# Layer 3's attention with smaller projection pieces, one a step, and router logits on VectorE

## The chip, the core and the metric

The kernel runs on one core of a Trainium2 chip, in one launch. The metric is the device time in microseconds. A core has five engines with queues of their own: PE (TensorE, matrix products into PSUM), DVE (VectorE, elementwise work and copies out of PSUM), ACT (ScalarE, activation functions), POOL (GpSimd) and SP, which here issues DMAs. PSUM has eight banks; one holds 128 x 512 numbers of 32 bits. All data are float32.

## The reference

Four layers in a row work on 8 samples of 256 channels by 1024 positions: two of convolutions, one of attention with a sparse feed-forward part, and layer 3, which the change concerns. A sample of layer 3 is 1024 tokens of 256 channels:

```python
t = t + _L3_attn_ref(_ln_t(t), qkv_w, qkv_b, proj_w, proj_b)
t = t + _L3_ffn_ref(_ln_t(t), router_w, w1, b1, w2, b2)
# attention: 8 heads of 32 channels, no softmax
scores = jnp.einsum('bnhd,bmhd->bhnm', q, k) * scale
s = jnp.square(scores + 5.0)
attn = s / jnp.sum(s, axis=-1, keepdims=True)
out = jnp.einsum('bhnm,bmhd->bnhd', attn, v).reshape(B, N, D) @ proj_w.T + proj_b
# feed-forward: 8 experts, two for each token
probs = jax.nn.softmax(tokens @ router_w.T, axis=-1)
rw, re = jax.lax.top_k(probs, 2)
# out = tokens + sum over the chosen experts of weight * (gelu(tokens @ w1 + b1) @ w2 + b2)
```

## The kernel before

Each layer is a Python generator; a layer's head (its loads, and what needs no space of the layer before) is issued beside the end of the layer before it. A list scheduler then orders the instructions of each engine: program order is its priority, an instruction can move ahead when it is ready earlier, and `pinned` ties one behind what was issued before it on its engine. Waits on tiles, and on space that another tile had, are set by the framework. Engines work their own queues in order.

**Attention of layer 3** is `fast3`. A sample has 32 steps: 2 halves of the queries (`hh`, 512 tokens each), 2 groups of four heads (`c`), 8 blocks of 128 keys (`kt`). In a step, four score matmuls (L2686), one for each head and each in 32 rows of the array, fill two pairs of PSUM banks, (s); ACT squares each pair (L2692) into `e`; one step later, four value matmuls (L2670), each in 32 columns of the array, add into the bank `A`. After eight steps `A` is multiplied by the inverse sums `r` into `o` (L2675), and after sixteen, the output projection (a whole pair, L78 and L2681) is added to the sample in `x`. PSUM holds three pairs with the tag S and two banks for A; every other user of PSUM in this stage takes a pair of S as well, through `pair` or `bank`.

Beside the steps of sample b, `between(b)` issues in this order: the routing of sample b - 1 (`Routes.route`: a norm, a transpose of the normed sample on PE (L2398), logits on PE (L78, mo_l), softmax, the two best experts by comparisons, and places by a running count with two small matmuls (mo_n)); the norm of sample b + 1 (`norm`: load, statistics on DVE, Ln and Exp on ACT, scaling, transposes into `xn`); and its projections (`projections`: q, k and v, then the denominators. Since no softmax is used, a row's sum follows from the Gram matrix of the keys, G, from the product of it with q, and from a sum over a head's channels, D.) `spread` deals them out evenly over 33 steps; a piece of projections takes a whole pair, and up to 16 matmul instructions. After sample 0's projections `routes.fill` presets the 19 MB lists that tokens are later sorted into. Sorting of a group of samples (`sort`) runs beside the samples 4 and 7.

Ahead of the first step come sample 0's transposes and projections. In the space that `own["k1"]` gets, and that the last layer's tiles leave, lies `kt`; `xt` and `xn` lie in a pool of their own, `one`, which the routing uses as well.

**The experts** are `fast3e`: 149 blocks of 128 tokens, two a pair. Their first 16 half pairs are issued together with the routing of the last sample, by due times (`by_time`: the stream that is due first goes next).

The few lines that set this order:

```python
ss = [pair("s") for _ in range(2)]                      # a step's score pairs
beside = [(between(b), 19 * (b + 1 < B) + (ROUTE if b else 6))]
spread((attention(b), 33), beside)                      # 33 slots a sample
by_time([[0, 1, some(all_pairs, lead)], [1, 1.1, routing]])   # fast3e, lead = 16
```

Of the kernel before, what the change touches and what calls it, by code (L numbers as in the profile page):

```python
# [897 lines left out]
class Fast:  # L898
# [114 lines left out]
    def token_norm_steps(self, dst, x, pool, placed=True):  # L1013
# [4 lines left out]
        for t in range(n):  # L1018
            self.nc.vector.tensor_scalar(
                dst[:, t, :], x[:, t, :], r[:, 0, t : t + 1], r[:, 1, t : t + 1], ALU.mult, ALU.add  # L1020
            )

# [1286 lines left out]
class Routes:  # L2309
# [28 lines left out]
    def load(self, wp):  # L2338

        net, nc = self.net, self.net.nc  # L2340
        self.wr = net.load(wp, "l3f_wr", "(k p) o -> p k o", p=P)
# [38 lines left out]
    def route(self, b, x, ones, pair):  # L2380
# [8 lines left out]
        yield from net.token_norm_steps(xn, x, two)  # L2389
# [3 lines left out]
        yield  # L2393
        xk = ones.tile([P, KC, N], F32, tag="xn", name="mo_xk")
        for c in range(KC):
            ps = pair("mo_xT").rearrange("p h n -> p (h n)")
            for t in range(NT):
                nc.tensor.transpose(ps[:, bass.ts(t, P)], xn[:, t, bass.ts(c, P)], net.ident)  # L2398
            nc.vector.tensor_copy(xk[:, c, :], ps)
            yield  # L2400

        pr = two.tile([P, NT, E8], F32, tag="pr", name="pr")
        for t4 in range(0, NT, 4):
            ps = pair("mo_l")[:, 0]
            for i in range(4):
                net.linear(ps[:, bass.ts(i, E8)], xk, self.wr, bass.ts(t4 + i, P), slice(0, E8))
            nc.vector.tensor_copy(pr[:, t4 : t4 + 4], ps[:, : 4 * E8].rearrange("p (t e) -> p t e", e=E8))
            if not t4:
                yield
        red = two.tile([P, NT], F32, tag="red", name="red")  # L2410
        nc.vector.tensor_reduce(red, pr, AX.X, ALU.max)
        nc.vector.tensor_tensor(pr, pr, each(red), ALU.subtract)
        yield
# [11 lines left out]
        nc.vector.tensor_tensor(eq, other, mine, ALU.is_equal)  # L2425
        nc.vector.tensor_tensor(eq, eq, self.before.unsqueeze(1).to_broadcast([P, NT, E8, E8]), ALU.mult)
# [6 lines left out]
        for i in range(2):  # L2433
# [3 lines left out]
            nc.vector.tensor_reduce(weigh[:, i], tmp, AX.X, ALU.add)  # L2437
        nc.vector.tensor_tensor(red, weigh[:, 0], weigh[:, 1], ALU.add)
# [5 lines left out]
        yield  # L2444

        ps = pair("mo_n")[:, 0]
# [10 lines left out]
        for t in range(NT):  # L2457
            nc.vector.tensor_tensor(place[:, t], cnt[:, 0, t], carry, ALU.add)
            nc.vector.tensor_tensor(carry, carry, cnt[:, 1, t], ALU.add)
        yield  # L2460
# [59 lines left out]
def fast3(net, io):  # L2520
# [4 lines left out]
    with ExitStack() as ctx, ExitStack() as tok, ExitStack() as att, ExitStack() as bef:  # L2525
# [3 lines left out]
        def pair(name):  # L2529
            return net.lent["pair"](name) if not own else own["S"].tile([P, 2, HF], F32, tag="S", name=name)  # L2530

        def bank(name):
            return pair(name)[:, 0]
# [31 lines left out]
        xs, xns, qs, ks, vs, rs = ({} for _ in range(6))  # L2565

        def norm(b):
            x = xs[b] = xpool.tile([P, NT, C], F32, tag="x", name="x")

            (nc.sync if b else nc.scalar).dma_start(out=halves(x), in_=tokens(io.src[b]))  # L2570
            yield
            xt = one.tile([P, NT, C], F32, tag="xt", name="xt")
            yield from net.token_norm_steps(xt, x, norms, b > 0)
            yield
            xn = xns[b] = one.tile([P, KC, N], F32, tag="xn", name="xn")
            for c in range(KC):
                ps = pair("xn")
                for t in range(NT):
                    nc.tensor.transpose(ps[:, t // 4, bass.ts(t % 4, P)], xt[:, t, bass.ts(c, P)], net.ident)
                nc.vector.tensor_copy(xn[:, c, :], ps.rearrange("p h n -> p (h n)"))  # L2580
                yield
            nc.gpsimd.tensor_tensor(x, x, bo.unsqueeze(1).to_broadcast([P, NT, C]), ALU.add)

        def projections(b):
            xn = xns.pop(b)
# [652 lines left out]
```

## Time and profile before

| | |
|---|---|
| runs, us | 4169.89, 4160.69, 4172.2; median 4169.89 |
| profiled execution | 4178.96 us; span of its instructions 4177.1 us |
| PE busy | 3826.0 us (92%) |
| DVE busy | 2298.4 us (55%) |
| ACT busy | 2260.1 us (54%) |
| POOL busy | 566.3 us (14%) |
| granted TensorE clock | 0.954 of full speed |
| attention of layer 3 | from 2819.65 to 3794.67 us, 975.0 us |

In the lists of instructions a line reads: source line, engine, operation, output tile and inputs, shapes, count; then busy time and the mean of one in ns; then the idle time of the engine just before these, and who ended it. A float32 matmul of the program stands as two instructions in the trace, a transpose as one. In the list of windows a line has the stretch, its length, busy us (and instructions) of PE, of its weight loads (PEld), of DVE, ACT and POOL, the granted clock, the share of the DMA engines' time, and GB/s. In the list of waits stand who waited, for whom, the sum in us, how often, and the longest. In the timeline stand start, duration, engine and instruction.

### The profile page before, as it was taken

What the parts mean: (1) busy time and instruction counts of PE and PEld (TensorE: products, weight loads), DVE (VectorE), ACT (ScalarE), POOL (GpSimd) and SP (SyncE); (2) the same over time, 40 slices, a digit from 0 to 9 for tenths busy, and PEclk for the clock granted to TensorE, in tenths of its full rate; (3) what the DMA queues carried; (4) which work ended last, traced back from release to release, by engine and by line L of the source; (5) the groups of instructions that cost most, each with busy time, mean ns of one, the idle gap of its engine ahead of it and who ended that gap; (6) DMA issues with size and microseconds to landing.
All of it is one profiled execution on the core that took longest, in us unless ns stands there. A gap on an engine that the chain in (4) does not pass through costs nothing. (4 is left out here: it accounts for less than half of the span.)

```text
span 4177.1 us, 51736 instructions
## 1 busy us (share of the span) xinstructions
PE 3826.0 (92%) x19430; PEld 1887.8 (45%) x19430; DVE 2298.4 (55%) x3994; ACT 2260.1 (54%) x3030; POOL 566.3 (14%) x646
## 2 busy tenths in 40 slices
PE   8999999999878787789999969989899999999987
PEld 3323333333334444454444526653344444346986
DVE  2398798798896489942222356841232333324445
ACT  4556555555553367734334346516566556666554
POOL 0000000000000000000000013430000050124753
PEclk9999999999998889889999979999999999999998
DMA  3313223223131568720000013430700040136676
GB/s 100 113 43 124 90 73 120 88 74 109 62 107 47 185 246 291 264 73 21 21 21 29 22 56 109 142 121 11 219 31 31 9 145 31 37 111 195 202 233 219
DMA packets 210069, 441.13 MB, mean 106 GB/s; under 512 B 22281, under 2 KB 132828, under 8 KB 197396
## 3 DMA queue, kind: packets, MB, share of 16 engines
q1 hardware_dynamic: 186708, 386.17, 28.1%
q0 software_dynamic: 19440, 46.45, 3.3%
q10 hardware_dynamic: 3664, 5.11, 0.4%
q8 instruction: 157, 2.57, 0.3%
q14 instruction: 100, 0.82, 0.1%
HBM read 282.30 MB, written 162.28 MB: 106 GB/s over the span
## 5 line engine op out<-in xcount | busy, mean ns | idle before, releaser
L2692 ACT ACTIVATE e<-s,five 128x1024 f32<-128x1024 f32 x512 | 539.3, 1111 | 280.0 <-PE s L2686 279.2
L1249 DVE SCALAR_TENSOR_TENSOR a<-hp,w_f_vec,a 128x961 f32<-128x961 f32 (+1 forms) x496 | 608.7, 1233 | 115.3 <-ACT a L1242 106.7
L2686 PE MATMUL s<-q,k 32*128 32x512 f32 x2048 | 349.1, 644 | 16.3 <-ACT e L2692 12.1
L1401 ACT ACTIVATE e<-s 128x1024 f32<-128x1024 f32 x256 | 250.2, 1023 | 79.4 <-PE s L1395 62.8
L2670 PE MATMUL A<-e,v 128*32 128x512 f32 x2048 | 279.0, 609 | 0.0
L1355 DVE TENSOR_TENSOR sum<-sum,e 128x1024 f32<-128x1024 f32 x192 | 230.6, 1220 | 87.2 <-ACT e L1401 87.2
L78 PE MATMUL pi<-xn,w_l_wpi 128*128 128x512 f32 x512 | 249.0, 629 | 19.2 <-ACT v L1283 10.0
L1359 PE MATMUL A<-e,va 128*32 128x512 f32 x2048 | 263.0, 610 | 0.0
L2686 PEld LDWEIGHTS s<-q,k 32*128 32x128 f32 x2048 | 111.4, 184 | 179.4 <-issue 96.2
L1395 PE MATMUL s<-q,k 32*128 32x512 f32 x1024 | 181.2, 650 | 2.5 <-ACT e L1401 2.5
L78 PEld LDWEIGHTS pi<-xn,w_l_wpi 128*128 128x128 f32 x512 | 96.7, 199 | 161.9 <-issue 118.2
L2839 PE MATMUL h<-xk,w 128*128 128x128 f32 x1192 | 150.7, 281 | 19.0 <-DVE xk L2825 19.0
L1706 PE MATMUL acc<-wt,z 128*64 128x192 f32 (+4 forms) x1344 | 128.9, 334 | 42.4 <-DVE wt L1761 42.0
L1026 POOL DMA_INDIRECT res<-y,to x149 | 148.4, 996 | 106.6 <-DVE y L2863 47.7
L2839 PEld LDWEIGHTS h<-xk,w 128*128 128x128 f32 x1192 | 148.3, 197 | 24.1 <-DVE xk L2825 19.3
L2808 ACT COPY w<-w_l3f_w 128x512 f32 x149 | 92.6, 625 | 119.6 <-PE h L2839 116.3
L1440 ACT ACTIVATE hp<-pi,pib 128x512 f32<-128x512 f32 x128 | 87.2, 690 | 127.3 <-PE pi L78 127.2
L1310 POOL MEMSET thrice<- 32x128 f32 x32 | 6.3, 196 | 1021.7 <-PE pe L1326 1021.6
L2859 PE MATMUL y<-w_l3f_w,hid 128*128 x596 | 142.8, 382 | 0.3 <-ACT hid L2845 0.3
L1026 POOL DMA_INDIRECT so<-xl,rows x128 | 129.9, 1015 | 93.0 <-issue 51.0
L1706 PEld LDWEIGHTS acc<-wt,z 128*64 128x64 f32 x1344 | 97.7, 151 | 89.5 <-DVE wt L1761 60.1
L1359 PEld LDWEIGHTS A<-e,va 128*32 128x32 f32 x2048 | 57.6, 111 | 174.2 <-issue 172.9
(407 smaller groups left out, 6966.5 us busy)
## 6 DMA issues: line engine op xcount, KB each, us to landing
row<-shifts SPq DMA_DIRECT2D x144, 512.0 KB
x<-d SPq DMA_DIRECT2D x31, 1024.0 KB
xs<-so SPq DMA_DIRECT2D x73, 260.0 KB
so<-zero SPq DMA_DIRECT2D x5, 3380.0 KB
thrice<-vimg SPq DMA_DIRECT2D x64, 256.0 KB
gated<-st SPq DMA_DIRECT2D x32, 512.0 KB
hc<-gated SPq DMA_DIRECT2D x32, 512.0 KB
xl<-mox SPq DMA_DIRECT2D x64, 256.0 KB
```

What stands on the lines that cost most here:

```text
L78: self.nc.tensor.matmul(ps, lhsT=w[:, i, m], rhs=src[:, i, cols], start=(i == 0), stop=(i == k - 1))
L1026: made = self.nc.gpsimd.indirect_dma_start(**args)
L1249: nc.vector.scalar_tensor_tensor(to, fr, taps(t_), to, ALU.mult, ALU.add)
L1355: nc.vector.tensor_tensor(half, half, e[j], ALU.add)
L1359: nc.tensor.matmul(state["A"][32 * h : 32 * h + 32, c, :], lhsT=vas[b][:, kt, c, 32 * h : 32 * h + 32], rhs=e[h // 2][:, h % 2, :], start= ...
L1395: nc.tensor.matmul(ss[h // 2][:, h % 2], lhsT=ks[b][32 * h : 32 * h + 32, bass.ts(kt, P)], rhs=qs[b][32 * h : 32 * h + 32, bass.ts(gq, HF) ...
L1401: nc.scalar.activation(es[i][j], ss[j], AF.Exp, scale=SCALE)
L1706: nc.tensor.matmul(acc[o, a * IMG : e * IMG], lhsT=zs[b][:, c, t, :], rhs=wt[:, c, (a - lo) * IMG : (e - lo) * IMG], start=False, stop=(t ...
L2670: nc.tensor.matmul(A[32 * h : 32 * h + 32], lhsT=v[:, kt, c * P + 32 * h : c * P + 32 * h + 32], rhs=e[:, h, :], start=first, stop=last,)
L2686: nc.tensor.matmul(ss[h // 2][:, h % 2], lhsT=k[32 * h : 32 * h + 32, c, bass.ts(kt, P)], rhs=q[32 * h : 32 * h + 32, c, bass.ts(hh, HF)], ...
L2692: nc.scalar.activation(e[:, 2 * j : 2 * j + 2], ss[j], AF.Square, scale=SCALE, bias=five)
L2839: nc.tensor.matmul(ps[:, j, m], lhsT=ws[j][:, k, bass.ts(m, P)], rhs=xk[:, j, k], start=(k == 0), stop=(k == KC - 1),)
```

## The change

- Score pairs: the three pairs of S are for scores alone. A has one bank instead of two, and one bank X serves every other use of PSUM in the stage. In the prologue, before X exists, those uses still take a bank of S.
- Pieces: every piece of the projections and of the output projection is half as large, one bank. They are issued as one stream, `products`, one piece a step (0.92 steps apart); a step with a piece of the output projection puts it off by one.
- The four heads' matmuls of scores and of values are pinned together, in the order 2, 3, 0, 1.
- The load and the norm of a sample are issued two samples ahead of its attention (`fetch` at step 8, `norm` at step 10), and its transposes (`turned`) between the pieces of `denominators`. `xt` shares a buffer with `prod`, and `xn` moves, both into `own["k1"]`. Samples 0 and 1 are normed and transposed before the first step.
- Routing of sample b - 1 runs beside the steps of b as a stream of its own, from step 3, 0.48 steps a part; `token_norm_pieces` gives its norm in small parts, and its first statistic is not pinned.
- The router's logits: 64 scalar_tensor_tensor with an accumulator on DVE for each sample, against a copy of the router's weights in every partition (`f3_wr`), in place of the transposes and matmuls on PE.
- The fill begins at step 6 of sample 0, and the experts' weights are loaded from step 5 of sample 7.
- In `fast3e` the last routing's parts are 0.26 apart instead of 1.1.

```diff
+    def token_norm_pieces(self, dst, x, pool):
...
+        for t in range(n):
+            nc.vector.bn_stats(st[:, t, :], x[:, t, :])
+            nc.vector.bn_aggr(mv[:, t, :], st[:, t, :])
+            if t % 2:
+                yield
+        yield
+        self.pinned(nc.scalar.activation(r[:, 0], mv[:, :, 1], AF.Ln, bias=self.eps5))
+        self.pinned(nc.scalar.activation(r[:, 0], r[:, 0], AF.Exp, scale=-0.5))
...
-    def route(self, b, x, ones, pair):
+    def route(self, b, x, ones, bank):
...
-        yield from net.token_norm_steps(xn, x, two)
+        yield from net.token_norm_pieces(xn, x, two)
         nc.sync.dma_start(out=self.normed[b], in_=xn)
         nc.gpsimd.tensor_tensor(x, x, xn, ALU.add)
         nc.sync.dma_start(out=self.sums[b], in_=x)
-        yield
-        xk = ones.tile([P, KC, N], F32, tag="xn", name="mo_xk")
-        for c in range(KC):
-            ps = pair("mo_xT").rearrange("p h n -> p (h n)")
-            for t in range(NT):
-                nc.tensor.transpose(ps[:, bass.ts(t, P)], xn[:, t, bass.ts(c, P)], net.ident)
-            nc.vector.tensor_copy(xk[:, c, :], ps)
-            yield
...
-            for i in range(4):
-                net.linear(ps[:, bass.ts(i, E8)], xk, self.wr, bass.ts(t4 + i, P), slice(0, E8))
...
+        for t in range(NT):
+            for e in range(E8):
+                nc.vector.scalar_tensor_tensor(
+                    junk, xn[:, t, :], 1.0, self.wr[:, e, :], ALU.mult, ALU.mult, accum_out=pr[:, t, e : e + 1]
+                )
+                if e % 2:
+                    yield
...
         def bank(name):
-            return pair(name)[:, 0]
+            if "X" in own:
+                return own["X"].tile([P, HF], F32, tag="X", name=name)
+            ps = own["S"].tile([P, 2, HF], F32, tag="S", name=name) if own else net.lent["pair"](name)
+            return ps[:, 0]
...
+        def fetch(b):
+            x = xs[b] = xpool.tile([P, NT, C], F32, tag="x", name="x")
+            (nc.sync if b else nc.scalar).dma_start(out=halves(x), in_=tokens(io.src[b]))
 
         def norm(b):
...
+            pool, tag = (own["k1"], "prod") if own else (one, "xt")
+            xt = xts[b] = pool.tile([P, NT, C], F32, tag=tag, name="xt")
+            yield from net.token_norm_pieces(xt, xs[b], norms)
+            nc.gpsimd.tensor_tensor(xs[b], xs[b], bo.unsqueeze(1).to_broadcast([P, NT, C]), ALU.add)
+
+        def turned(b, h, c):
+            if b not in xns:
+                xns[b] = own["k1"].tile([P, KC, N], F32, tag="xn", name="xn")
+            ps = bank("xn")
+            for t in range(4):
+                nc.tensor.transpose(ps[:, bass.ts(t, P)], xts[b][:, 4 * h + t, bass.ts(c, P)], net.ident)
+            nc.vector.tensor_copy(xns[b][:, c, bass.ts(h, HF)], ps)
...
+            def together(h, ins):
+                if h != LATEST[0]:
+                    net.pinned(ins)
...
-        own["S"], own["A"] = io.pool(att, "f3s", 3, PSUM), io.pool(att, "f3v", 2, PSUM)
+        own["S"], own["A"] = io.pool(att, "f3s", 3, PSUM), io.pool(att, "f3v", 1, PSUM)
...
+        fetch(1)
+        for h in range(2):
+            for c in range(KC):
+                turned(0, h, c)
+        second = norm(1)
         for _ in projections(0):
+            next(second, None)
+        for _ in second:
             pass
+        for h in range(2):
+            for c in range(KC):
+                turned(1, h, c)
+        for _ in denominators(0):
+            pass
+        own["X"] = io.pool(att, "f3o", 1, PSUM)
...
+            if b + 1 < B:
+                parts.append(products(b + 1))
+                streams.append([at + (3 if b else 0), 0.92, parts[-1]])
+            if b + 2 < B:
+                streams.append([at + 8, 1, later(1, (fetch(n) for n in (b + 2,)))])
+                streams.append([at + 10, 0.5, norm(b + 2)])
+            if b:
+                streams.append([at + 3, 0.48, routed(b - 1)])
+            if b == 0:
+                streams.append([at + 6, 1, routes.fill()])
             if b == B - 1:
-                bef.close()
...
+                streams.append([at + 5, 2, loads()])
...
-        by_time([[0, 1, some(all_pairs, lead)], [1, 1.1, routing]])
+        by_time([[0, 1, some(all_pairs, lead)], [1, 0.26, routing]])
```

## The prediction

> **What bounds the kernel now.** I read the page's slices first (PE at 8 to 9 tenths nearly everywhere, so a stage has to be looked at on its own), then the busy windows by sample, the groups of instructions inside the attention of layer 3, the waits there, and last the timeline. Attention runs from the first score matmul at 2819.65 us to the last value matmul's end at 3794.67 us: 975.0 us for 8 samples of 32 steps. The score matmuls' starts in the timeline give 119.0, 138.9, 124.5, 125.2, 126.4, 124.5, 126.2 and 90.2 us for the samples. One window and the groups:
>
> ```profile
> 3065.00:3187.00 122.00, 121.75 (x730) 51.20 (x723) 38.56 (x107) 75.97 (x77) 9.38 (x4) 1.00 0.07 27
> ...
> L2692 ACT ACTIVATE e<-s,five 128x1024 f32<-128x1024 f32 x512 | 539.3, 1111 | 280.0 <-PE s L2686 279.2
> L2686 PE MATMUL s<-q,k 32*128 32x512 f32 x2048 | 349.1, 644 | 16.3 <-ACT e L2692 12.1 <-DVE cnt L2451 1.8 <-DVE x L2681 1.8
> L78 PE MATMUL mo_l<-w_l3f_wr,mo_xk 128*128 128x8 f32 x224 | 27.2, 257 | 0.0
> L2398 PE MATMUL mo_xT<-ident,mo_x 128*128 128x128 f32 x112 | 15.3, 280 | 0.0
> ```
>
> In a sample PE is busy 121.75 of 122 us, VectorE 38.56, ScalarE 75.97; ScalarE spends 279.2 us waiting for scores. So TensorE is the bound, yet not every step is: the next lines are one step with a large piece of projections in it.
>
> ```profile
> 3143.36 1.14 PE L2686 MATMUL s<-q,k 32*128 32x512 f32 x8
> 3143.46 1.11 ACT L2592 ACTIVATE q<-qk,w_l_vec 128x1024 f32<-128x1024 f32 x1 [2.53 <-PE qk L78]
> 3144.43 1.07 PE L2670 MATMUL A<-e,v 128*32 128x512 f32 x8
> 3144.59 2.12 ACT L2692 ACTIVATE e<-s,five 128x1024 f32<-128x1024 f32 x2
> 3145.42 3.70 PE L78 MATMUL qk<-xn,w_l_wq 128*128 128x512 f32 x8
> ```
>
> Start to start: scores 1.07 us, values 0.99, piece 3.63 (the next scores start at 3149.05). Such a step is PE's, 5.7 us, and ScalarE idles 2.5 us in it; a step without a piece (3118.38, 3120.77, 3122.84, 3125.28: 2.07 to 2.44 us) is held by ScalarE's two squares, 2.22 us. PE work bunched in some steps leaves idle PE in others.
>
> **What the skill says.** "Perfetto Trace Analysis", section on the Tensor Engine instruction, says the end of a matmul is estimated and not observed; so I count from start to start. "TensorEngine Tiling (Array Packing)", Key Properties: changing the tiling mode drains TensorE. The trace agrees: in a piece the matmuls follow each other every 0.43 us, 8 x 0.427 = 3.41, and the piece takes 3.63, so each change costs about 0.22 us, and twice as many half pieces pay it twice. "VectorE: DVE Perf Modes", Two Vector instructions with no wait between them: an op that writes its accumulator is two instructions. The router of layer 2 shows the very form that the change brings to layer 3:
>
> ```profile
> 2435.82 0.42 DVE L2127 SCALAR_TENSOR_TENSOR junk<-xn,w_f_wr 128x256 f32<-128x256 f32 x1 [0.58 <-ACT xn L2115]
> 2436.17 0.08 DVE L2127 DVE_READ_ACCUMULATOR junk<-xn,w_f_wr 128x1 f32 x1
> 2436.36 0.42 DVE L2127 SCALAR_TENSOR_TENSOR junk<-xn,w_f_wr 128x256 f32<-128x256 f32 x1
> ```
>
> That is 0.538 us each, start to start. "TensorE: Matmul & The Clock Gate", the part on queue depths, has ScalarE and VectorE as strict FIFO; in the trace one statistic waiting for its sample stopped VectorE for 15.5 us and PE behind it for about 14 (first line below).
>
> ```profile
> DVE tn_s L1003 <- DMA x<-d: 17.1, 2, 15.5
> SPq L2570 <- DMA mos<-x: 11.6, 4, 3.6
> ...
> 2785.35 4.70 DVE L2242 SCALAR_TENSOR_TENSOR s<-yg,m,s 128x256 f32<-128x256 f32 x8
> 2790.08 0.32 SPq L2246 DMA_DIRECT2D d<-s  x1
> ...
> 3835.00:3855.00 20.00, 18.85 (x132) 17.47 (x131) 16.39 (x73) 10.35 (x28) 9.52 (x13) 1.00 0.43 130
> 3855.00:3875.00 20.00, 20.00 (x144) 18.96 (x144) 7.77 (x16) 11.39 (x30) 14.16 (x19) 1.00 0.48 152
> ```
>
> The first pair of lines is the stall and the chain that feeds it; the second pair is layer 2's last but one sample, still being summed and stored when layer 3 begins; the last pair is the start of the experts, where PE is full again soon after the last sample's routing.
>
> **Attention, part by part.** A sample's PE work, start to start. Scores and values: 32 x (1.07 + 1.00) = 66.2, kept. Keys and queries: 4 pieces of 3.63 become 8 of 4 x 0.427 + 0.22 = 1.92: 14.5 to 15.4. Values' projection: 2 of 3.65 to 4 of 1.95: 7.3 to 7.8. Transposes of keys, and of the normed sample: 2 of 1.02 to 4 of 0.60 each: 2.05 to 2.4 twice. Gram products: 3.77 to 2 x 2.05. Products and weights: 2 of 1.91 to 4 of 1.06, each 3.83 to 4.24. Output projection: two of 3.85, plus two more switches where it cut a step's scores in two (2 + 6 matmuls, 1.05 more each), 9.8, to 4 x 1.95 = 7.8, the scores being pinned together. Routing: transposes 2 x 1.02 and logits 2 x 1.88 go, 5.8; the counts, 0.6, stay. Sum before 120.0 in a full sample (125.2 measured, so 5 lost to steps that ScalarE holds); after 115.1. Of that, spread over 32 steps of 3.6 us, ScalarE has 2.57 (2.22 and 11 us of halves and exponentials a sample), so no step is ScalarE's any more and the 5 us go too.
>
> VectorE gains 64 x 0.538 = 34.4 us a sample, loses 2.9, and pays some 2 for halves: 40 to 74 of 118 us. It is hidden by PE on average. At its tightest, five steps that hold a norm (6.6 us), 4.2 logits a step (2.24 us) and a copy a step (0.7) want 21.3 us of 18. Behind VectorE's queue wait the copies out of the one bank that all pieces now share, and the product that frees the single value bank (0.69, before the next eight steps' values); PE waits for both. The trace of before has neither wait. Bounds: 0, as a copy has 2.07 us of scores and values to hide in and the logits can run ahead in earlier steps; 3.3, all that the five steps are short. I take 2 us a sample. The load of two samples ahead reuses the buffer that routing frees: pool add 4.5, store 3.9 (the second line of the pair), load 7.0 (issued 2988.10, used 2995.14), 15.5 us or 4.4 steps after routing's norm, done about 6 steps into a sample; with 3.4 us of statistics that is step 11.5, and ScalarE's pinned Ln stands at 12.5. In sample 4 SP also holds a sort's loads: there the load was issued 12.4 us after the store (3344.8, 3357.2) instead of 3.9, a step late once. I take 1 us a sample; bounds 0 and 4, and more than that is rival (c). The fill's 19 MB, which hold SP for some 60 us from 2920 on, move to steps 6 to 13 of the first sample, where the third sample's load is issued before them; so the 14 us stall of sample 1 goes.
>
> Samples: 114.5 + 2 for the first (no routing), 5 x 118, 112.7 + 3 for the seventh (no transposes ahead), and for the last 90.2 less 5.8, less 2.1 for the cut scores, plus 3 spilled pieces, 86. Sum 908: **67 us saved**, and 42 to 87 with the bounds. At nothing: the experts' weights, now loaded at step 5 of the last sample (4 MB, some 14 us at the 300 GB/s that windows of this stage reach, with 27 steps to hide in); the pool adds and stores, the same as before.
>
> **Before the first step.** Both norms and both transposes are now ahead of attention. From the v matmuls' end to the first score took 14 us; now the second sample's transposes, 2.4, and half pieces, 1.3 and about 2, come on. And xn moves into the pool of kt: the kernel's address map has sample 6's s of layer 2 at bytes 193,568 to 201,760, and xn at 196,032, just after where kt began. So the first copies wait for that store: sums right behind the norm, 2782.4 to 2786.4, stored 3.9 later, PE starts at 2791.3 instead of 2784.25, 7 us. Sum **+14**, bounds 5 (gaps filled by scores) and 25.
>
> **The last routing, beside the experts.** Nothing of attention hides its 34.4 us of logits. The due times put 32 parts at 0.26, 8.3 half pairs, between them; a pair of experts is 1.8 + 0.44 + 1.73 = 3.95 us of PE but 1.6 of VectorE, so VectorE needs 8.3 x 0.538 x 7.7 + 4.15 x 1.6 = 41 us for 4.15 pairs. Before, the same 41 us after 3814 had room for about 7.9 pairs beside the routing's own PE work. 3.7 pairs x 3.95 = **+15**; bounds 0, if experts' copies go first, and 25. No cover is left later: PE is full to 4140.
>
> Sum: -67 + 14 + 15 = -38. Against the profiled execution, 4178.96 us (span 4177.1), that is 4141; the median of the runs, 4169.89, lies 0.2% below it, and the same 38 off gives **4132**.
>
> **Rivals.** (a) Everything packs: attention at its PE sum, 888, is -87, prologue +8, last routing +5: -74, 4096. For it: matmuls follow without a gap in the large pieces today. Against: three engines' in-order queues would have to fit. (b) It gives back what it takes: -47 + 22 + 25, no change, 4170; for it, both ends are serial and PE there has nothing else. (c) Slower: VectorE's statistics for two samples ahead stand unpinned in its queue before the load has landed. Everything behind them, the copies out of the shared bank above all, waits, and PE with them; the trace has this once at 14 us. For five samples with a reused buffer 72 us in all: -67 + 72 + 29 = +34, 4204. It decides from 7.6 us per such sample on; the second line of the pair shows SP already held by that store. Against: 1 step of slack by my count. (d) That the scheduler undoes the spreading, pieces bunching again, is part of (b).
>
> **How the numbers follow.** Forecast 0.50 (own range 4105 to 4158), (a) 0.20, (b) 0.12, (c) 0.18. About 0.3%, 12.5 us, is what a measurement of this kernel can tell. Forecast and (a) give 0.70, (b)'s lower side 0.04 and the forecast's upper edge takes 0.02: faster 0.72, same 0.08, slower 0.20. The range 4090 to 4195 leaves out the best of (a) and the worst of (c).
>
> **What would show it.** Right: steps of 3.5 to 3.7 us in all samples, mo_xT and mo_l gone from PE, ScalarE's wait for scores far below 279 us; first score near 2834; attention near 908; few experts' matmuls beside the last sample's logits. Wrong: VectorE waiting for x by more than some 10 us in all, PE waiting for copies of the shared bank, or an experts' stage as long as before (382 us).

## The result, and the profile after

The changed kernel takes **4287.5 us** (median of 4 runs, 4277.3 to 4299.4); the kernel before, run beside it, takes 4165.3. The ratio is 1.0295 (95%: 1.026 to 1.033), 122 us slower, where 38 us faster was forecast. The profiled execution is 4277.3 us, its span 4275.6.

Layer 3 begins 23 us earlier in the profile of after than in that of before, so only stages of layer 3 are compared. `bo` is its first matmul, a product with the weights of the output projection.

| stage | before | after | difference | forecast |
|---|---|---|---|---|
| from the start of `bo` to the first score | 49.9 | 77.3 | +27.4 | +14 |
| attention | 975.0 | 1066.6 | +91.6 | -67 |
| after the last value matmul | 382.5 | 385.3 | +2.8 | +15 |

The three sum to 121.8 us, the whole difference of the medians. By samples, attention is now 112.6, 140.4, 143.0, 143.2, 147.1, 143.1, 138.1 and 99.2 us. The first, which has no routing beside it, came out 4 us better than forecast; the next six 22 to 29 us worse each, the last 13. Two windows of after show why to look at them apart (first sample, then sample 2; busy times of PE, weight loads, DVE, ACT, POOL, then the granted clock):

```profile
2823.00:2936.00 113.00, 111.55 (x662) 39.20 (x660) 19.94 (x40) 78.04 (x81) 4.69 (x2) 1.00 0.06 19
3077.00:3220.00 143.00, 125.86 (x696) 45.52 (x692) 70.01 (x242) 78.65 (x84) 9.32 (x3) 0.93 0.06 23
```

PE is idle 17 of 143 us, and its busy time is longer than before's 121.75 although it has less work: the clock is 0.93. VectorE, which PE waits for, is busy only half the time. The groups and the waits of after:

```profile
L2728 ACT ACTIVATE e<-s,five 128x1024 f32<-128x1024 f32 x512 | 543.8, 1112 | 326.6 <-PE s L2721 326.5
L2706 PE MATMUL A<-e,v 128*32 128x512 f32 x2048 | 282.7, 621 | 69.6 <-DVE o L2712 69.6
L2419 DVE SCALAR_TENSOR_TENSOR junk<-mo_x,w_f_wr 128x256 f32<-128x256 f32 x512 | 250.5, 489 | 16.1
```

```profile
DVE tn_r L1037 <- ACT tn_r L1036: 114.2, 15, 15.9
...
PE A L2706 <- DVE o L2712: 69.6, 8, 9.7
...
PE v L78 <- DVE v L2622: 38.0, 11, 11.6
...
PE xn L2603 <- DVE xn L2604: 21.9, 1, 21.9
```

Neither wait of the two in the middle, for `o` and for the copy of v, exists in the trace of before. ScalarE now waits longer for scores (326.5 us, before 279.2), the opposite of what the prediction names as a sign of success. One such stall, in order of time:

```profile
3104.56 0.17 DVE L1037 SCALAR_TENSOR_TENSOR tn_r<-tn_m,tn_r 128x8 f32<-128x8 f32 x1 [14.99 <-ACT tn_r L1036]
3104.82 2.67 DVE L1040 TENSOR_SCALAR mo_x<-x,tn_r 128x256 f32<-128x256 f32 x8
...
3107.58 4.64 POOL L2412 TENSOR_TENSOR x<-x,mo_x 128x2048 f32<-128x2048 f32 x1 [61.33 <-DVE mo_x L1040]
...
3107.87 4.63 DVE L2419 SCALAR_TENSOR_TENSOR junk<-mo_x,w_f_wr 128x256 f32<-128x256 f32 x1
...
3110.84 1.06 PE L2706 MATMUL A<-e,v 128*32 128x512 f32 x8
...
3123.28 0.42 DVE L2419 SCALAR_TENSOR_TENSOR junk<-mo_x,w_f_wr 128x256 f32<-128x256 f32 x1
3123.63 0.69 DVE L2712 TENSOR_TENSOR o<-A,r 128x512 f32<-128x512 f32 x1
...
3124.37 1.94 PE L2706 MATMUL A<-e,v 128*32 128x512 f32 x8 [9.48 <-DVE o L2712]
```

Read from the bottom. PE waits 9.48 us for `o`, because the one value bank is free only then. `o` itself had its data at 3111.9, when the value matmuls of 3110.84 ended. But it stands in VectorE's queue behind 26 logits, from 3107.4 to 3123.6. They run as late as this, in one train, because the routing's norm first waited 15 us for its Ln on ScalarE, which is pinned behind squares (before, this wait was 2.4 us in most samples). The scheduler, which orders each engine's queue, let the logits go ahead of `o`; it looks as if it did not foresee that wait, but its own times are not in the trace. And one logit takes 4.63 us instead of 0.42: it ends 0.3 us after the addition on GpSimd. Then the value matmuls take 1.94 us instead of 1.06: the granted clock there is 0.5.

### The profile page after: what moved, and what is told of

Its sections match the earlier page's. It is cut to its first block, busy times and chain, and to the rows that moved or that the text cites. A ratio compares the mean times of both kernels' runs of the same rounds, so it can differ in the third digit from the quotient of the medians.

```text
span 4275.6 us, 52079 instructions
## 1 busy us (share of the span) xinstructions
PE 3795.2 (89%) x19046; PEld 1827.2 (43%) x19046; DVE 2539.1 (59%) x5074; ACT 2276.9 (53%) x3078; POOL 571.0 (13%) x646
## 5 line engine op out<-in xcount | busy, mean ns | idle before, releaser
L2728 ACT ACTIVATE e<-s,five 128x1024 f32<-128x1024 f32 x512 | 543.8, 1112 | 326.6 <-PE s L2721 326.5
L2721 PE MATMUL s<-q,k 32*128 32x512 f32 x2048 | 338.2, 657 | 1.0 <-ACT e L2728 1.0
L2419 DVE SCALAR_TENSOR_TENSOR junk<-mo_x,w_f_wr 128x256 f32<-128x256 f32 x512 | 250.5, 489 | 16.1
L78 PE MATMUL pi<-xn,w_l_wpi 128*128 128x512 f32 x512 | 238.7, 607 | 14.9 <-ACT u L1523 9.2
L1416 PE MATMUL s<-q,k 32*128 32x512 f32 x1024 | 178.3, 646 | 2.5 <-ACT e L1422 2.5
L2928 PE MATMUL h<-xk,w 128*128 128x128 f32 x1192 | 150.9, 281 | 23.1 <-DVE xk L2914 23.1
L78 PE MATMUL v<-w_l_wv,xn 128*128 128x256 f32 x512 | 132.7, 410 | 38.0 <-DVE v L2622 38.0
L2721 PEld LDWEIGHTS s<-q,k 32*128 32x128 f32 x2048 | 96.9, 189 | 158.3 <-issue 138.2
L2706 PEld LDWEIGHTS A<-e,v 128*32 128x32 f32 x2048 | 41.6, 109 | 271.1 <-issue 180.0
```

What stands on the lines that cost most here:

```text
L78: self.nc.tensor.matmul(ps, lhsT=w[:, i, m], rhs=src[:, i, cols], start=(i == 0), stop=(i == k - 1))
L2419: nc.vector.scalar_tensor_tensor(junk, xn[:, t, :], 1.0, self.wr[:, e, :], ALU.mult, ALU.mult, accum_out=pr[:, t, e : e + 1])
L2706: nc.tensor.matmul(A[32 * h : 32 * h + 32], lhsT=vs[b][:, kt, c * P + 32 * h : c * P + 32 * h + 32], rhs=e[:, h, :], start=first, stop=last,),
L2721: nc.tensor.matmul(ss[h // 2][:, h % 2], lhsT=ks[b][32 * h : 32 * h + 32, c, bass.ts(kt, P)], rhs=qs[b][32 * h : 32 * h + 32, c, bass.ts(h ...
L2728: nc.scalar.activation(e[:, 2 * j : 2 * j + 2], ss[j], AF.Square, scale=SCALE, bias=five)
L2928: nc.tensor.matmul(ps[:, j, m], lhsT=ws[j][:, k, bass.ts(m, P)], rhs=xk[:, j, k], start=(k == 0), stop=(k == KC - 1),)
```

## The experiments

Twelve kernels were run. All are in this table; the ratio is to the kernel before on the same chip. (Runs 1 to 3 had a chip on which the kernel before takes 4214 us, so totals that were expected of them are to be read as ratios to 4165.3.) "Idle" is PE's idle time within attention, in gaps of over 0.3 us; "half clock" is a sum over unbroken groups of like matmuls of the time by which they exceed the usual one of their kind, where that is over 30% and the granted clock was below full speed. At full clock, groups of scores are stretched as well, mostly since their weight loads wait for ScalarE's squares: by 17 us in the kernel before, 34 us in run 3, 12 us in run 4 and 1 to 4 us in the others, which neither column counts. The start of layer 3 differs by up to 47 us between runs and chips, so stages are given too.

| kernel | ratio (95%) | attention | idle | half clock | `bo` to first score | after attention |
|---|---|---|---|---|---|---|
| before | 1 | 975.0 | 15.1 | 6.9 | 49.9 | 382.5 |
| changed | 1.0295 (1.0260 to 1.0330) | 1066.6 | 118.6 | 37.3 | 77.3 | 385.3 |
| 1 logits in order | 1.0121 (1.0072 to 1.0170) | 1002.0 | 64.1 | 28.7 | 79.1 | 399.7 |
| 2 logits on PE | 1.0534 (1.0488 to 1.0579) | 1194.6 | 75.0 | 112.6 | 79.0 | 397.6 |
| 3 two value banks | 1.0254 (1.0214 to 1.0294) | 1053.7 | 125.5 | 12.5 | 77.2 | 399.9 |
| 4 before, logits on VectorE | 1.0147 (1.0117 to 1.0177) | 1041.2 | 100.4 | 25.1 | 49.7 | 382.4 |
| 5 norms, routing in order | 1.0077 (1.0051 to 1.0103) | 964.5 | 39.3 | 18.1 | 79.1 | 399.0 |
| 6 as 2, norm later | 1.0442 (1.0412 to 1.0471) | 1152.1 | 56.6 | 89.7 | 79.6 | 378.3 |
| 7 as 1, transposes early | 1.0091 (1.0062 to 1.0119) | 997.8 | 65.0 | 23.8 | 60.9 | 390.5 |
| 8 both repairs (5 and 7) | 1.0030 (1.0018 to 1.0041) | 965.9 | 39.5 | 19.4 | 63.8 | 393.7 |
| 9 as 8, additions on VectorE | 1.0023 (1.0014 to 1.0032) | 974.2 | 57.1 | 11.0 | 58.2 | 394.2 |
| 10 as 6, in order | 1.0324 (1.0304 to 1.0344) | 1092.2 | 22.4 | 63.2 | 77.5 | 376.8 |
| 11 as 9, loads in order | 0.9992 (0.9981 to 1.0004) | 925.5 | 18.2 | 1.5 | 58.8 | 414.8 |
| 12 as 11, last routing on PE | 0.9900 (0.9879 to 0.9922) | 929.6 | 18.0 | 3.9 | 57.9 | 381.5 |

**Theories.** 1: order in VectorE's queue. 2: the single value bank. 3: VectorE has too much to do. 4: half pieces through one shared bank are too slow.

**Run 1: the logits in program order.**

```diff
-                nc.vector.scalar_tensor_tensor(
+                net.pinned(nc.vector.scalar_tensor_tensor(
                     junk, xn[:, t, :], 1.0, self.wr[:, e, :], ALU.mult, ALU.mult, accum_out=pr[:, t, e : e + 1]
-                )
+                ))
```

> Changed kernel, each of the 64 logits of a sample kept in program order on VectorE, nothing left out. Theory 1 (order: the scheduler let some 36 logits go ahead of the product o and of the copies out of the shared bank, and PE stands for them): the stalls of PE at A (69.6 us) and at v (38.0 us) go for the most part and the granted clock of a routed sample returns to 1.00; attention falls from 1067 to 950-990 us, total 4170-4215. Theory 2 (the single value bank stalls PE whatever stands in VectorE's queue) and theory 3 (VectorE has too much to do): the same logits have to be done in the same samples, so PE's stalls move but remain, total within 25 us of the changed kernel's 4287.

Nothing but the order was changed, and attention lost 65 us, half of PE's idle time with it. That is theory 1; theories 2 and 3 expected no more than 25. But 1002 lies above the 950 to 990 expected. About 10 logits still stand before `o` in the program's order as well, one of them of 4.6 us. And with the trains gone, statistics of the norm two samples ahead wait for x, 4 to 17 us in each of five samples, and in sample 4 PE stood 11.5 us at v behind that: rival (c) of the prediction.

**Run 2: logits on PE, all else of the change kept.**

```diff
-        junk = one.tile([P, C], F32, tag="junk", name="junk")
...
+            for c in range(KC):
+                ps = bank("mo_xT")
+                for t in range(4):
+                    nc.tensor.transpose(ps[:, bass.ts(t, P)], xn[:, 4 * h + t, bass.ts(c, P)], net.ident)
+                nc.vector.tensor_copy(xk[:, c, bass.ts(h, HF)], ps)
...
+        for t2 in range(0, NT, 2):
+            ps = bank("mo_l")
```

> Changed kernel with layer 3's router logits back on PE (transposes, products and copies in half pieces of the shared bank); single value bank, half pieces, spread order all kept, nothing left out. PE gets 5.8 to 7 us a sample back (about 45 us), VectorE loses some 28 us a sample. Theories 1 and 3 (VectorE's logits are the cause, by order or by amount): PE's stalls at A and v all but vanish, total 4165-4220. Theory 4 (half pieces through one shared bank and the single value bank are too slow in themselves): stalls remain above 60 us, total 4260 or more.

Stalls above 60 us and a total above 4260 are what theory 4 expected. Theories 1 and 3 have the stalls at A and v vanish, which they did but for 2 us, and missed the total. An attention longer by 128 us was named by none. PE's idle time fell to 75, and 113 us went at half clock. Of the stalls, 41 us (at mo_xT) were statistics of the norm two samples ahead, waiting for x in front of the copies out of the shared bank: rival (c) again, which the trains of logits had covered in the changed kernel. Another 26 us, in five samples, came behind a small comparison of the routing, which took 4.1 us instead of 0.2 beside GpSimd's addition of the bias:

```profile
3260.90 4.52 POOL L2602 TENSOR_TENSOR x<-x,w_f_bo 128x2048 f32<-128x2048 f32 x1 [68.56 <-DVE xt L1040]
...
3261.39 4.18 DVE L2456 TENSOR_SCALAR chosen<-rank 128x64 f32<-128x64 f32 x2
...
3267.64 1.11 PE L2639 MATMUL kT<-ident,k 128*128 128x128 f32 x4 [5.25 <-DVE v L2628]
```

Runs 6 and 10 follow this up.

**Run 3: the banks of before.**

```diff
-        own["S"], own["A"] = io.pool(att, "f3s", 3, PSUM), io.pool(att, "f3v", 1, PSUM)
+        own["S"], own["A"] = io.pool(att, "f3s", 3, PSUM), io.pool(att, "f3v", 2, PSUM)
...
-        own["X"] = io.pool(att, "f3o", 1, PSUM)
```

> Changed kernel with the banks of the kernel before: two value banks, no bank of its own for the other pieces, which take turns in the three score pairs again; logits on VectorE in the changed order, nothing left out. Theory 2 (single value bank): the stall at A goes, total down by 70 us or more (at most 4215). Theory 1: the stall at A (70 us) goes here too, since the next eight values no longer need o, but every late copy now holds one of the score pairs, so the stalls at v and xn become stalls at s: total 4225-4275. Theory 4 (shared single bank): total down by 40 or more.

With two value banks the stall at A is gone, and PE waits as long for the copies of v, which stand in the same trains. From the waits of this run:

```profile
PE v L78 <- DVE v L2622: 108.6, 11, 21.4
```

Attention is 13 us shorter. Theory 2 falls: the bank only decides which matmul does the waiting. The stall came at v, not at s as theory 1 had it; groups of scores are stretched too, by 34 us. Read as a ratio to 4165.3 us, theory 1's range is 1.014 to 1.026, and the run is at its upper end.

**Run 4: the kernel before with the logits alone** (samples 0 to 5, eight to a part; with the logits of all samples there, the experts' weights, 32.1 KB a partition, don't fit into the 24.5 KB that this kernel has left).

```diff
+        if b < B - 2:
+            pr = two.tile([P, NT, E8], F32, tag="pr", name="pr")
+            junk = one.tile([P, C], F32, tag="junk", name="junk")
...
+                    if e == E8 - 1:
+                        yield
+        else:
```

> Kernel before with one part of the change alone: logits of samples 0 to 5 on VectorE, eight to a part and five parts more to a routing, those of 6 and 7 still on PE; two value banks, full pieces, norm one sample ahead, nothing left out. PE loses 5.8 us of work in six samples (35 us). Rival 'banks and pieces': the logits hide, ratio 0.992 to 1.000. Theory 1 (order): trains of logits stand in front of copies here too and hold the score pairs: ratio 1.005 to 1.02. Amount: 1.005 or more as well, with no idle time of VectorE while PE waits.

The ratio lies in theory 1's range; the path does not. ScalarE's timeline, and PE's line behind it:

```profile
3111.00 0.26 ACT L2425 ACTIVATE pr<-pr 128x64 f32<-128x64 f32 x1 [15.61 <-DVE pr L2423]
3111.16 3.10 ACT L2703 ACTIVATE e<-s,five 128x1024 f32<-128x1024 f32 x3
...
3112.32 2.08 PE L2697 MATMUL s<-q,k 32*128 32x512 f32 x4 [14.70 <-ACT e L2703]
```

No copy that PE waits for is late. The softmax's Exp is pinned on ScalarE and waits for the last of 64 logits in one train, which ended at 3110.4; the squares stand behind it and PE behind these, 13.5 to 14.9 us in each of six samples. So the logits cost 66 us in attention even with the old banks, old pieces and old norm: their 30 us in one train are late for whatever is queued behind their result, on either engine. VectorE is not idle during these stalls, it works on the logits, so this run does not tell theory 1 from theory 3.

**Run 5: all of VectorE's norm and routing in order**, routing a step later, norm of two samples ahead three steps later.

```diff
         red = two.tile([P, NT], F32, tag="red", name="red")
-        nc.vector.tensor_reduce(red, pr, AX.X, ALU.max)
+        net.pinned(nc.vector.tensor_reduce(red, pr, AX.X, ALU.max))
...
-                streams.append([at + 10, 0.5, norm(b + 2)])
+                streams.append([at + (13 if b else 10), 0.5, norm(b + 2)])
...
-                streams.append([at + 3, 0.48, routed(b - 1)])
+                streams.append([at + 4, 0.48, routed(b - 1)])
```

> Changed kernel with every VectorE instruction of the norms and of the routing kept in program order (not the logits alone), the routing begun one step later and the norm of two samples ahead three steps later; nothing left out. Theory 1 (order in VectorE's queue, the load of x included): the 64 us of PE stalls that were left with only the logits in order fall under 25, attention from 1002 to 940-965 us, and the total is 40 us or more below that run (ratio to before 1.002 or less). Rival (VectorE simply has too much to do, or the single banks are too few): stalls stay above 50 us, total within 15 us of that run (ratio 1.009 to 1.015).

Attention is 964.5 as theory 1 expected, for the first time below before's 975; idle time is 39, not under 25, and the ratio missed 1.002, with 17 to 21 us of it behind attention (399.0, against 382.4 and 378.3 in runs 4 and 6 of the same chip). Of the idle time left, 21.3 us come at one place, xn, five times:

```profile
3159.09 4.58 POOL L2596 TENSOR_TENSOR x<-x,w_f_bo 128x2048 f32<-128x2048 f32 x1 [39.20 <-DVE xt L1040]
3159.33 4.62 DVE L2419 SCALAR_TENSOR_TENSOR junk<-mo_x,w_f_wr 128x256 f32<-128x256 f32 x1
...
3164.81 0.68 DVE L2636 COPY kt<-kT 128x512 f32<-128x512 f32 x1
...
3165.55 1.12 PE L2603 MATMUL xn<-ident,xt 128*128 128x128 f32 x4 [4.53 <-DVE kt L2636]
```

A logit that starts while GpSimd adds lasts until that addition ends; two more logits and the copy of kt follow, and PE has waited 4.53 us for the shared bank. In the changed kernel this happened in all seven routings of attention (4.62 or 4.63 us each). The Trainium skill states it: "SBUF — State Buffer", Who interferes with whom, has a VectorE instruction with two inputs from SBUF contend with a GpSimd instruction that reads SBUF, since both need a pair of ports that is locked for one of them. The traces agree, with 4.62 us instead of 0.42.

**Run 6: logits on PE, norm later.** The edit is run 2's with the norm's line of run 5.

> Changed kernel with the logits on PE, as in the earlier run with a ratio of 1.053, and one thing more: the norm of two samples ahead three steps later, so that its statistics do not stand in VectorE's queue before x has landed. Theory c (statistics before the load, in front of the copies out of the shared bank, and the half clock that follows): the stalls at mo_xT and kT (68 us) and most of the 116 us at half clock go; attention from 1195 to 960-1020, ratio 1.000 to 1.017. Rival (more and smaller pieces cut the scores apart and keep PE at half clock by themselves): attention stays above 1120, ratio 1.04 or more.

Attention is 43 us shorter, not 175 or more, but the wait itself was not removed: free to move, the statistics went ahead in VectorE's queue as before.

```profile
3152.72 0.75 DVE L1030 BATCH_NORM_STATS2 tn_s<-x 128x6 f32<-128x256 f32 x2 [8.15 <-DMA x<-d]
...
3153.79 0.67 DVE L2422 COPY mo_xk<-mo_xT 128x512 f32<-128x512 f32 x1
```

So this run couldn't separate the two, and run 10 was made.

**Run 7: the first sample's transposes early**, as in the kernel before, on top of run 1.

```diff
         yield from norm(0)
+        yield
+        turn = []
+        for c in range(KC):
+            ps = net.lent["pair"]("xn")
...
+        xns[0] = one.tile([P, KC, N], F32, tag="xt", name="xn")
+        for c in range(KC):
+            nc.vector.tensor_copy(xns[0][:, c, :], turn[c].rearrange("p h n -> p (h n)"))
         yield HOLD
```

> Logits in order as in the run with a ratio of 1.012, and the first sample's normed x transposed before the layer takes over the space of the one before it, as in the kernel before (in place, over xt); nothing left out. Theory P1 (in the changed kernel the first transposes' copies stand in VectorE's queue behind layer 2's last summation, which waits for gathers): from bo to the first score 79 us falls to 55-62, total 18 to 24 us below that run (ratio 1.007). Rival P2 (the second sample's norm, transposes and the half pieces cost the 27 us): 72 us or more, total within 7 us.

From `bo` to the first score 79 (79.1 and 79.6 in runs 5 and 6 of the same chip) fell to 60.9, as P1 expected; the ratio is 1.0091, two points of a thousand above its 1.007. The changed kernel's VectorE timeline shows what it undid:

```profile
2775.06 0.48 DVE L2263 SCALAR_TENSOR_TENSOR s<-yg,m,s 128x256 f32<-128x256 f32 x1 [11.16 <-DMA yg<-pk,idx]
...
2782.96 0.48 DVE L2263 SCALAR_TENSOR_TENSOR s<-yg,m,s 128x256 f32<-128x256 f32 x1 [0.42 <-DMA yg<-pk,idx]
2783.55 2.59 DVE L2604 COPY xn<-xn 128x512 f32<-128x512 f32 x4
```

The copies of xn stand behind layer 2's last summation, eight pieces that each wait for a gather. In the kernel before, the copies of xn stood ahead of it and only those of v behind it. The change traces the transposes after HOLD, hence after all of layer 2.

**Runs 8 and 9: both repairs, then the additions to x on VectorE.** Run 8 combines 5 and 7, with no pins in the routing beside the experts and before attention. Run 9 adds:

```diff
-        nc.gpsimd.tensor_tensor(x, x, xn, ALU.add)
+        for t in range(0, NT, 2):
+            keep(nc.vector.tensor_tensor(x[:, t : t + 2], x[:, t : t + 2], xn[:, t : t + 2], ALU.add))
+            yield
```

and the same for the bias.

> The two repairs together, nothing left out: VectorE's instructions of norms and routing in program order (as in the run with a ratio of 1.008; left free in the routing beside the experts and before attention), and the first sample's transposes before the layer takes over its space. If the pieces add: attention 964 as there, from bo to the first score 61, after attention 383-388: 31 us below that run, ratio 0.998 to 1.003. Rival (what is gained at one place is lost at the next): ratio above 1.004.

> As the run before it in this list, but with both additions to x (of mo_x and of the bias) on VectorE, in four pieces each, instead of one 4.6 us instruction on GpSimd; nothing left out. Theory L (a logit, which reads two operands from SBUF, is held for the whole of GpSimd's addition, 4.6 us instead of 0.42, and a copy out of the shared bank behind it keeps PE waiting): the logits of 4.6 us go, the stalls at xn (21 us) and A (8 us) fall under 10 together, attention from 964 to 930-945, ratio 0.990 to 0.996. Rival (VectorE, 70 of 130 us busy, gets 5.5 us a sample more to do): stalls stay or grow, attention 960 or more, ratio 1.000 or more.

Run 8: attention is where the repair had it, the stretch ahead of it 3 us longer; behind attention 393.7 instead of 383 to 388, so the ratio is 1.003, at the upper end. In run 9 no logit is longer than the others (in run 8, 13 are), and six of seven routed samples are shorter or within 2 us: 117.8, 125.9, 124.4, 121.7, 119.7 and 83.4, in run 8 123.3, 129.3, 129.5, 126.7, 118.0 and 90.4. In these samples that is theory L, and against "too much to do": VectorE got more work and PE waited less at xn and A, 6 us in all instead of 29. The totals are the rival's, for sample 4 takes 166.1 instead of 136.6:

```profile
3408.47 0.43 DVE L1030 BATCH_NORM_STATS2 tn_s<-x 128x6 f32<-128x256 f32 x1 [41.24 <-DMA x<-d]
```

```profile
3342.36 46.57 SPq L2525 DMA_DIRECT2D xl<-mox  x15
3388.97 0.47 SPq L2412 DMA_DIRECT2D mox<-mo_x  x1
3389.49 0.43 SPq L2416 DMA_DIRECT2D mos<-x  x1
...
3400.86 0.47 SPq L2593 DMA_DIRECT2D x<-d  x1
```

SP had 15 loads of the sort ahead of the store that frees the buffer of x and of the load that fills it; VectorE stood 41 us before the statistics. Rival (c) again, in SP's queue.

**Run 10: logits on PE, everything in order** (run 5 with the logits on PE, in the pieces of run 2).

> Changed kernel with the logits on PE again and VectorE's norm and routing instructions in program order, so that the statistics of two samples ahead can no longer stand before the load of x; nothing left out. In the run with a ratio of 1.044 they still did. Theory c: the stalls at mo_xT (41 us) go, half clock with them, attention from 1152 to 1000-1060, ratio 1.008 to 1.022. Rival (small pieces between scores keep PE at half clock): stalls go, yet 60 us or more are still lost at half clock, attention 1070 or more, ratio 1.025 or more.

The stalls at mo_xT are gone, idle time is 22 us, and yet attention is 1092, 128 us more than in run 5: the rival. PE's timeline, in which no matmul waits:

```profile
3148.90 1.12 PE L2728 MATMUL s<-q,k 32*128 32x512 f32 x2
3149.95 1.06 PE L78 MATMUL mo_l<-w_l3f_wr,mo_xk 128*128 128x8 f32 x8
3150.94 1.32 PE L2728 MATMUL s<-q,k 32*128 32x512 f32 x4
3152.19 1.94 PE L2713 MATMUL A<-e,v 128*32 128x512 f32 x8
3154.05 1.88 PE L78 MATMUL mo_l<-w_l3f_wr,mo_xk 128*128 128x8 f32 x8
3155.86 2.07 PE L2728 MATMUL s<-q,k 32*128 32x512 f32 x2
```

Small pieces cut the scores in 2, 4 and 2, and without a gap between them the clock halves at 3152. Half clock is only 45 of the 128 us. The transposes and logits are themselves 48 us of PE, and they cut the scores into 333 groups instead of 280; a group takes 1.1 us, whether it holds two matmul instructions or eight, so that is some 59 us more (an estimate from these counts), and idle time is 17 us less. So the rest of the change is not good by itself: with logits in small pieces on PE it is no faster than the changed kernel (1.032 against 1.0295).

**Run 11: the sort's loads in order.**

```diff
-                nc.sync.dma_start(
+                self.net.pinned(nc.sync.dma_start(
                     out=xl[:, :, :C], in_=self.normed[s][:, t : t + 1].to_broadcast([P, 2, C])
-                )
+                ))
```

> As the run with both additions on VectorE (ratio 1.002), and the sort's loads kept in program order on SP, so that 15 of them no longer go ahead of the store and the load of x in sample 4; nothing left out. If that load (VectorE waits 41 us for it, PE 39) is all that spoils that run: sample 4 falls from 166 to 125-130 us, attention from 974 to 932-942, total 35 us below the kernel before at best: ratio 0.990 to 0.996. Rival (the sort then holds up what follows it, or the time comes back after attention): ratio 0.998 or more.

Sample 4 is 123.5, attention 925.5, 50 us below the kernel before. The total is that of before all the same, the rival's case: behind attention 414.8, 32 us more. In that stretch PE waits 26.0 us for xk behind VectorE (before 19.0), 15.3 us for the experts' rows and 7.3 us for the counts' input, neither of which it waits for in the kernel before.

**Run 12: the last routing as in the kernel before** (the edit without the smaller changes that its expectation names).

```diff
+        if spare is None:
...
+        else:
+            xk = spare.tile([P, NT, C], F32, tag="x", name="mo_xk").rearrange("p t c -> p (t c)").rearrange("p (k n) -> p k n", k=KC)
...
-        routing = routes.route(B - 1, xs[B - 1], one, bank)
+        routing = routes.route(B - 1, xs[B - 1], one, bank, xpool)
```

> As the run with the sort's loads in order (ratio 0.999, attention 925 us, 415 us after it), with the last sample's routing, which runs beside the experts, done as in the kernel before: logits on PE, the addition on GpSimd; the routing of the last but one begun at the same step and spread a little closer, and only the first sort's loads held in order; nothing left out. Theory T (what attention won came back as 32 us behind it: logits and additions on VectorE there stand before the experts' copies, PE waits at h and at the counts): after attention 380-388 us, total 25-32 us below that run, ratio 0.991 to 0.994. Rival (the experts simply start in the same place because their tables come from the last sorts): after attention above 400, ratio above 0.996.

Behind attention 381.5, and 4127.6 us in all: **ratio 0.990 (0.988 to 0.992), 1% faster than the kernel before**. Its sample 2:

```profile
3043.00:3167.00 124.00, 120.36 (x696) 43.86 (x692) 68.83 (x250) 78.33 (x84) 0.64 (x2) 0.99 0.07 27
```

VectorE is as busy as in the changed kernel's 143 us window (68.8 and 70.0), and PE is idle under 4 us instead of 17. Theory 3 falls with this line, and so do 2 and 4: the single value bank, the half pieces and the shared bank are all still there.

By samples, attention takes 113.7, 117.8, 124.4, 124.4, 123.3, 121.7, 119.7 and 84.7 us. Of the 45 us below the kernel before, 21 are in sample 1 (138.9 before), where the kernel before has a statistic wait for its load and PE stand 11 us; samples 2 to 5 together give 7. So with the queues in order most of the gain forecast for the ordinary samples (124.5 to 118) is still not there.

## Why the prediction was wrong

**What bounds the kernel:** right. PE's sum was nearly right as well: the first sample was forecast at 116.5 and took 112.6, and the changed kernel's attention without idle time and half clock is 1066.6 - 118.6 - 37.3 = 911 us, run 12's 929.6 - 18.0 - 3.9 = 908, against the 888 that the prediction gives as the bare sum. The 20 to 23 us that are missing are about one term: the prediction has the cut scores vanish, "the scores being pinned together", but there are 281 groups of scores in the changed kernel and 280 in run 12 for 256 steps, at 1.05 us each by its own count.

**The step that failed** is VectorE's in "Attention, part by part": "I take 2 us a sample", bounds 0 and 3.3. It measured 118.6 us of idle PE, nearly all behind VectorE, 17 for each of seven routed samples, and 30 us more at half clock than before. The prediction compared loads step by step (21.3 us wanted, 18 there) and took running ahead as a relief: "the logits can run ahead in earlier steps". Running ahead was the harm. A queue in order serves what the scheduler put first, and the scheduler put 26 logits before an `o` and some 33 before a copy of v that PE needs. Putting them in order, with nothing else changed, gave back 65 us (run 1). The second missed term is in the same part: "the pool adds and stores, the same as before", at nothing. They are the same; what runs on VectorE beside them is not, and each addition holds a logit for 4.2 us (changed kernel and run 5; gone in run 9). The prediction cites the skill on VectorE's queue and not on this port.

**The clock** was in no step. PE's stalls cost more than their length: with 104 us more of idle time, 30 us more were lost at half clock. The trace of before had this price in it. What the prediction reads there as a stall of PE of "about 14" us is 11.2 us of stall and the rest half clock behind it, and it came by way of ScalarE's pinned Ln:

```profile
2995.69 0.30 ACT L1008 ACTIVATE tn_r<-tn_m,eps 128x8 f32<-128x8 f32 x1 [11.81 <-DVE tn_m L1006]
...
2997.29 2.08 PE L2686 MATMUL s<-q,k 32*128 32x512 f32 x4 [11.18 <-ACT e L2692]
2999.29 1.94 PE L2670 MATMUL A<-e,v 128*32 128x512 f32 x8
```

**The load two samples ahead**, 1 us a sample with "a step late once" in sample 4, was right for the changed kernel: VectorE waits for x 5 us there. Rival (c) names this mechanism for the slower case, and it was not what made this kernel slow; it appeared when the trains were gone or shorter (4 to 17 us a sample in run 1, 8 to 20 in run 6, 41 us once in run 9). So the direction of that rival was met by another cause, and at 4204 us it was too small.

**Before the first step**: +14 forecast, +27.4 measured. The 7 us for the store of sample 6's s was the wrong wait: PE stood 21.9 us because the copies stand behind the last summation. Run 7 got 18 back. Of the rest, 60.9 against 49.9, the second sample's transposes and half pieces that the prediction lists make 5.7; the other 5 us are open, and neither was tested by itself. (The prediction's terms add to 12.7 us, not 14.)

**The last routing**: +15 forecast, +2.8 measured, near the lower bound of 0. Its reason, experts' copies going first, holds in part: in the trace they go between the logits, and PE waits 23.1 us for xk, before 19.0. It is luck as much as a right price: in runs 5, 7, 8, 9 and 11, which have the logits there on VectorE too, this stage takes 390 to 415 us; on the chips of runs 5 and 7 and of runs 8 and 9 it takes 377 to 382 with that routing on PE (runs 4, 6 and 10). Run 12 undoes several things there at once, so which of them cost that is not separated.

Open: how much of run 12's 45 us in attention is due to the moved norm and fill (21 us are in sample 1), to the spread of the pieces and to the logits. Run 4 has the logits in trains and run 10 the spread with small logit pieces on PE, and both lose by that. Nor was VectorE's wait for ScalarE's pinned Ln, 13 to 16 us in six of seven routings, taken away.

## What to carry to other kernels

Moving work to an engine that is idle half the time moves it into a queue: look for what PE needs that will stand behind it, at the place where the scheduler puts it and at the time when its own inputs come, rather than compare sums. Tie such filler behind the copies and products that free PSUM, on the engine and on its DMA queue. And price a stall of PE at more than its length, since the clock falls with it (here 37 us at half clock beside 119 us of stalls). Where a scheduler may cut a group of scores with small pieces, count the cuts as well: each is a whole group's time.

## What the runs showed of the hardware

- A VectorE multiply with two operands in SBUF took 4.62 to 4.65 us instead of 0.42 when it started within GpSimd's 4.6 us addition, and ended 0.3 us after it: all 7 in the attention of the changed kernel, 12 in that of run 8. It is not the multiply alone: in run 2 a comparison of 128 x 64 numbers took 4.03 to 4.08 us instead of 0.19, five times.
- A group of score matmuls took 1.12 us with two instructions (one head) and 1.14 us with eight (four heads) in the timelines of after and of run 10: cutting a step's scores in three triples their time.
- PE fell to half clock (value matmuls 1.94 instead of 1.06 us): the granted clock stayed at 0.5 for 3.5 to 5.9 us after each of the seven stalls of 8.6 to 9.7 us at A in the changed kernel, and for a stretch of 3.4 us after each of five stalls of 1.9 us. The Trainium skill, "TensorE: Matmul & The Clock Gate", Part 1, has the clock fall after an idle window of about 3.4 us; here shorter stalls were enough, and in run 10 it fell nine times with no idle gap of PE in the 10 us before, eight of them for 10 us or more, while PE ran short pieces of mixed shapes. That the shapes are the reason is not shown; run 5, without these pieces, loses 18 us at half clock, run 10 63 us.
- The logits follow each other every 0.47 us; in layer 2, whence the prediction took 0.538, they do not. 64 of them are 30 us, not 34.4.
